# A long 2-D convolution on one Trainium2 core: shifted copies of the input loaded in twelve pieces instead of two

## The chip, the cores and the metric

The kernel runs on one core of a Trainium2 chip (trn2). The metric is the device time of one execution in microseconds (us). The kernel before takes 16334.61 us, the median of three runs (16324.06 to 16345.95). The profile shown below is of one further execution.

The engines are named as the profile names them: PE is TensorE (PEld its weight loads), DVE is VectorE, ACT is ScalarE, POOL is GpSimd, SP is SyncE, which here only issues DMAs. Each engine works through its own list of instructions in the order in which they stand, and an instruction that waits holds up all that stand behind it on that engine.

## The reference

Two residual layers, each on a group-normed input `x` of shape (4, 512, 512, 16), all in float32:

```python
x = x + conv0(gn(x))     # a rational 2-D filter of 512x512 taps, 16 -> 16 channels, by FFT, causal
x = x + conv1(gn(x))     # a 3x3 convolution, cosine-normed, arccos, gated by tanh of norms

def conv0(x, h0, numerators, denumerator):
    h = irfft2(rfft2(pad(numerators)[0]) / rfft2(pad(denumerator)))
    H = h0 + rfft2(h, s=(1024, 1024))
    X = rfft2(x, s=(1024, 1024))
    Y = einsum('...hwi,ijhw->...hwj', X, H)
    return irfft2(Y)[..., :512, :512, :]
```

The change lies in the first layer, in the part that multiplies the two spectra.

## The kernel before

The kernel works in phases: the filter's spectrum, the input's transform along one axis, the **convolution phase** (`conv_phase`, lines 696 to 960), and a last phase with the way back and the second layer. Only the convolution phase is touched. It works through 513 rows, one for each frequency of the first axis (the first frequency counts as two, 0 and the highest). In a row n:

- `load_x`, `load_g` (L748, L736) fetch the row's input `x` (256 KB) and filter `g` (1024 KB).
- `x_part` (L777, PE) turns `x` into 128 frequencies in two pieces of PSUM, `px`, of two images each. Each is copied into `xe[:, 0]` (L727 on DVE or L729 on ACT).
- `x_late` (POOL) stores `xe[:, 0]` into a buffer `xf_d` in device memory (the **first store**, L791, 448 KB), forms a second half `xl` by two pairs of multiplications into `xu` (L798), a multiplication (L799) and an addition (L800), and stores that behind the first (the **second store**, 448 KB). `xf_d` then holds 256 positions by 1024 numbers; there are four such buffers.
- `load_xe` (L815, SP) reads it back as eight copies `xe[:, t]`, copy t shifted by 16 t positions. Copy 0 is there already. Copy 4 is a shift by half and is made by two ACT copies, `half_shift` (L809), the second of them from `xl`. Copies 1 to 3 and 5 to 7 are loaded, in two DMAs of 1536 KB each.
- `g_part` (L829, PE; "pg") turns the filter into `gh`: four groups of 8 matmuls, each group into two PSUM tiles of which there are three buffers, evicted on ACT or DVE.
- `mix` (L845, PE; "pm") multiplies `xe` by `gh`: 128 matmuls in four blocks of 32, each block into a PSUM tile `pm`. There are **two** such buffers; a block is evicted into `yf` by DVE (the first block of a row in the steady state) or ACT (the other three).
- `over_q` (L866, PE; "pz") transposes `yf` in four groups. ACT copies half of a group out (`zq`, L873) and DVE adds and subtracts (five operations, L874 to L878) into `z`. After the fourth group POOL forms `zd` and `z` (L882, L884).
- `over_g` (L903, PE; "py") goes on from there, ACT evicts `yo`, POOL stores it (L914).

`px`, `pz` and `py` share three PSUM buffers. `xe` has three buffers, `xl` one, and `g`, `x`, `gh`, `yf` and `z` two. `evict` (L724 to L729) gives every third PSUM copy to DVE and the others to ACT.

The program text lays these out as a software pipeline (`step`, L923 to L957): in step n it interleaves, quarter by quarter, `mix` of row n, `g_part` of row n+1, `over_q` of row n-1, the second `px` of row n+2 with its `x_late`, `half_shift` of row n+2, the first `px` of row n+3, and `over_g` of row n-2. `load_xe(n + 1)` stands at the head of the step. The text is not the last word on the order, though. A list scheduler decides at build time, from its own estimates of what is ready when, in which order each engine gets its instructions, and the hardware keeps to that order. It also puts each SP DMA on one of eight semaphores in turn, so a DMA waits until the one issued eight earlier has landed. In the kernel before the scheduler has kept the text's interleaving: from row 3 on to the last rows, PE runs one block of 32 mix matmuls, 8 of pg, 4 of pz and then px or py, four times a row.

Of the kernel before, what the change touches and what calls it, by code (L numbers as in the profile page):

```python
# [46 lines left out]
P = 128  # L47
N = 512
B = 4
C = 16  # L50
# [7 lines left out]
XF = F * 2 * B  # L58
XP = XF + 128
# [131 lines left out]
def load_const(nc, pool, cst, name, shape=None):  # L191
    src = cst[name]
    t = pool.tile(list(src.shape), F32, name=f"c_{name}")
    nc.sync.dma_start(out=t, in_=src)
    return t
# [10 lines left out]
def bc(ap, axis, shape):  # L206
    return ap.unsqueeze(axis).to_broadcast(shape)
# [488 lines left out]
def conv_phase(tc, cst, g_d, x_d, y_d):  # L696
    nc = tc.nc
    with ExitStack() as ctx:
# [15 lines left out]
        late = load_const(nc, cp, cst, "late").rearrange("p (v f) -> p v f", v=3)  # L714

        xf_d = [tc.dram_tile([16 * C, XP], F32, name=f"xf_d{n}") for n in range(4)]
# [4 lines left out]
        state = {}  # L721
# [9 lines left out]
        def load_g(n):  # L731
            rc, r, plane = rows[n]
            g = io.tile([P, C, 8 * C], F32, name="g")
            t, w = g.rearrange("p j x -> p (j x)"), C * 8 * C
            if plane is None:
                nc.sync.dma_start(out=t, in_=dram(g_d[rc], r, 0, [GP, P], [1, w]))  # L736
            else:
                for to, at in ((0, (0, 96)[plane]), (64, (64, 32)[plane])):
                    nc.sync.dma_start(out=t[to : to + 32], in_=dram(g_d[rc], r, at * GP, [GP, 32], [1, w]))
                    nc.gpsimd.memset(t[to + 32 : to + 64], 0.0)  # L740
            state["g", n] = g

        def load_x(n):
            rc, r, plane = rows[n]
            x = io.tile([P, B, 8 * C], F32, name="x")
            t, w = x.rearrange("p b x -> p (b x)"), B * 8 * C
            if plane is None:
                nc.sync.dma_start(out=t, in_=dram(x_d[rc], r, 0, [w, P], [1, w]))  # L748
            else:
                nc.gpsimd.memset(t[S:], 0.0)  # L750
                nc.sync.dma_start(out=t[:S], in_=dram(x_d[rc], r, plane * S * w, [w, S], [1, w]))
            state["x", n] = x
# [16 lines left out]
        def x_part(n, b):  # L769

            if b == 0:

                state["xe", n] = xep.tile([P, 8, F, 2, 2, 2], F32, name="xe")
            if b % 2 == 0:
                state["px"] = ps_f.tile([P, 2, F, 2], F32, name="px", tag="full")
            px = state["px"]
            nc.tensor.matmul(px[:, b % 2].rearrange("p f c -> p (f c)"), state["x", n][:, b],  # L777
                             state["dfs", n], start=True, stop=True)
            if b % 2:
                evict(state["xe", n][:, 0, :, b // 2], px.rearrange("p k f c -> p f c k"))  # L780
            if b == B - 1:
                del state["x", n], state["dfs", n]

        def x_late(n):

            xe = state["xe", n][:, 0]
            fl = xe.rearrange("p f h c k -> p f (h c k)")

            def store(half, t):
                at = slice(C, P) if half == 0 else slice(0, P - C)  # L790
                nc.gpsimd.dma_start(out=xf_d[n % 4][half * P :, :XF][at], in_=t[at].rearrange("p f x -> p (f x)"))  # L791

            store(0, fl)
            xl = xlp.tile([P, F, 2, 2, 2], F32, name="xl")
            u = xlp.tile([P, F, 2, 2, 2], F32, name="xu")
            for c in range(2):
                for h in range(2):
                    nc.gpsimd.tensor_mul(u[:, :, h, c], xe[:, :, h, 1 - c], bc(late[:, 1 + c], 2, [P, F, 2]))  # L798
            nc.gpsimd.tensor_mul(xl.rearrange("p f h c k -> p f (h c k)"), fl, bc(late[:, 0], 2, [P, F, 8]))  # L799
            nc.gpsimd.tensor_add(xl.rearrange("p f h c k -> p (f h c k)"),  # L800
                                 xl.rearrange("p f h c k -> p (f h c k)"),
                                 u.rearrange("p f h c k -> p (f h c k)"))
            store(1, xl.rearrange("p f h c k -> p f (h c k)"))
            state["xl"] = xl

        def half_shift(n, half):

            dst, src = ((slice(0, 64), state["xe", n][64:, 0]), (slice(64, P), state["xl"][:64]))[half]
            nc.scalar.copy(state["xe", n][dst, 4].rearrange("p f h c k -> p (f h c k)"),  # L809
                           src.rearrange("p f h c k -> p (f h c k)"))  # L810

        def load_xe(n):
            src = xf_d[n % 4]
            for t in (1, 5):
                nc.sync.dma_start(  # L815
                    out=state["xe", n][:, t : t + 3].rearrange("p t f h c k -> p t (f h c k)"),
                    in_=bass.AP(tensor=src.tensor, offset=src.offset + t * C * XP,
                                ap=[[XP, P], [C * XP, 3], [1, XF]]),
                )

        def g_part(n, j):


            if j % 4 == 0:
                state["pg"] = [ps_g.tile([P, 4, F], F32, name=f"pg{c}", tag="pg") for c in range(2)]
            g, pg = state["g", n], state["pg"]
            for c in range(2):
                half = slice(64 * c, 64 * c + 64)
                nc.tensor.matmul(pg[c][:, j % 4], g[half, j], dg[half], start=True, stop=True)  # L829
            if j == 3:  # L830
                state["gh", n] = ghp.tile([P, F, 2, C], F32, name="gh")
            if j % 4 == 3:
                for c in range(2):
                    evict(state["gh", n][:, :, c, j - 3 : j + 1], pg[c].rearrange("p j f -> p f j"))
            if j == C - 1:
                del state["g", n]

        def mix(n, g):

            if g % 8 == 0:  # L840
                state["pm"] = ps_m.tile([P, 8, 8, 2 * B], F32, name="pm")
            xe, gh, pm = state["xe", n], state["gh", n], state["pm"]
            for q in range(4):
                f = g + 32 * q
                nc.tensor.matmul(  # L845
                    pm[32 * q : 32 * q + 32, g % 8], gh[:, f].rearrange("p c j -> p (c j)"),
                    xe[:, :, f].rearrange("p t h c k -> p t (h c k)"), start=True, stop=True,
                )
            if g == 7:

                state["y", n] = yp.tile([P, 16, 32, 4], F32, name="yf")
            if g % 8 == 7:
                evict(state["y", n][:, :, g - 7 : g + 1].rearrange("p t g x -> p g t x"),
                      pm.rearrange("p g t (h x) -> p g (t h) x", h=2))
            if g == 31:
                del state["xe", n], state["gh", n]
# [65 lines left out]
        def step(n):  # L922


            def row(k):
                return 0 <= n + k < n_rows

            if row(3):
                load_x(n + 3)
            if row(2):  # L930
                load_g(n + 2)
            if row(1):
                load_xe(n + 1)
            for k in range(4):
                if row(0):
                    for g in range(8):
                        mix(n, 8 * k + g)
                if row(1):
                    for j in range(4):
                        g_part(n + 1, 4 * k + j)  # L940
                if row(-1):
                    for t in range(4):
                        over_q(n - 1, 4 * k + t)
                if row(2) and k == 0:
                    for m in range(2, B):
                        x_part(n + 2, m)
                    x_late(n + 2)
                if row(2) and k >= 2:
                    half_shift(n + 2, k - 2)
                if row(3) and k == 1:  # L950
                    turn_x(n + 3)
                if row(3) and k == 3:
                    for m in range(2):
                        x_part(n + 3, m)
                if row(-2) and k in (1, 2):
                    for m in range(2):
                        over_g(n - 2, 2 * (k - 1) + m)  # L957

        for n in range(-3, n_rows + 2):
            step(n)  # L960
# [479 lines left out]
```

## Time and profile before

| what | value |
|---|---|
| median of three runs | 16334.61 us |
| the profiled execution | 16344.5 us, its span on the core 16342.7 us |
| convolution phase, first to last mix matmul | 4654.0 to 13530.0 us: 8876 us for 513 rows, 17.30 us each |
| busy in that stretch | PE 7896.23, PEld 6185.06, DVE 4756.47, ACT 4655.71, POOL 5717.71 us |
| DMA in that stretch | 87% busy on the mean, 328 GB/s |
| granted PE clock in that stretch | 0.98 of full speed |

The profile can be asked for groups of instructions by line, for who waited for whom (what an engine's instruction waited for last, in us, how often, and the longest), for each engine's busy time in stretches, and for a timeline, whose rows give start and duration in us, engine, line, operation, what is written from what, how many alike were put together, and in brackets how long the engine had stood idle and what ended that. In the trace a float32 matmul is two records, so that a block of 32 mix matmuls appears as x64. "issue" means that nothing the profile shows was waited for.

### The profile page before, as it was taken

Reading aid. Unit: us, or ns where it says so; the run is one execution under the profiler, and the core shown is the slowest. Engines: PE = TensorE matmul, PEld = TensorE weight load, DVE = VectorE, ACT = ScalarE, POOL = GpSimd, SP = SyncE. Lnnn points to the kernel's source line nnn. Section 1 sums busy time; section 2 is a strip of 40 time slices with the busy share of each in tenths; the row PEclk is TensorE's granted clock in tenths of the full one; section 3 lists DMA queues with packets and bytes.
Section 4 is the critical chain, followed back from the end, with each engine's and each line's share of the span. In section 5 each row is a group of like instructions: output and inputs, shape, how many; then the busy total and the mean of one; then the engine's idle time right before and its main releaser. Section 6 shows DMA issues by size and latency. Waiting matters only on the chain. (4 is left out here: it accounts for less than half of the span.)

```text
span 16342.7 us, 538107 instructions
## 1 busy us (share of the span) xinstructions
PE 14869.0 (91%) x232588; PEld 10969.0 (67%) x232588; DVE 10396.8 (64%) x20763; ACT 8766.8 (54%) x17007; POOL 10169.4 (62%) x9645
## 2 busy tenths in 40 slices
PE   7999999999988888888888888888888888988888
PEld 5555555554566667766666676667666667877777
DVE  8999999984545555555555555555555552457887
ACT  4666666653345555555555555555555551027888
POOL 7777777763456666666666666666666660247766
PEclk8999999999999999999999999999999999989999
DMA  4888888888878888888888888888888886884531
GB/s 138 239 244 249 241 242 245 245 241 261 250 276 329 323 329 329 329 330 329 329 331 324 330 328 327 328 325 327 330 331 328 326 325 236 319 297 164 168 109 67
DMA packets 2914643, 4542.93 MB, mean 278 GB/s; under 512 B 126114, under 2 KB 2094460, under 8 KB 2801422
## 3 DMA queue, kind: packets, MB, share of 16 engines
q1 hardware_dynamic: 2703070, 3836.37, 67.9%
q0 software_dynamic: 172336, 605.00, 9.3%
q10 hardware_dynamic: 36864, 67.13, 1.2%
q8 instruction: 1831, 30.00, 0.7%
q14 instruction: 542, 4.44, 0.1%
HBM read 3030.71 MB, written 1477.31 MB: 276 GB/s over the span
## 5 line engine op out<-in xcount | busy, mean ns | idle before, releaser
L845 PEld LDWEIGHTS pm<-xe,gh 128*32 128x32 f32 x131328 | 2001.2, 111 | 1446.2 <-issue 1163.4
L845 PE MATMUL pm<-xe,gh 128*32 128x64 f32 x131328 | 2373.7, 222 | 650.1 <-issue 314.8
L829 PE MATMUL pg<-c_dg,g 64*128 64x128 f32 x32832 | 2599.4, 289 | 308.3 <-ACT gh L729 192.5
L874 DVE TENSOR_TENSOR z<-zq,pz 128x256 f32<-128x256 f32 x2052 | 861.6, 420 | 2952.0 <-ACT zq L873 2950.0
L829 PEld LDWEIGHTS pg<-c_dg,g 64*128 64x128 f32 x32832 | 2134.2, 190 | 573.3 <-ACT gh L729 245.9
L729 ACT COPY gh<-pg 128x512 f32<-128x512 f32 x2567 | 1446.9, 585 | 1296.4 <-PE pg L829 1293.9
L459 PE MATMUL pt<-ev_in,c_todd 128*128 128x512 f32 x4096 | 1924.7, 609 | 9.5 <-DMA ev_in<-g_d 9.5
L389 DVE RECIPROCAL dn<-dn 128x256 f32<-128x256 f32 x1024 | 1722.9, 1724 | 17.6
L390 POOL TENSOR_TENSOR sp<-m,dn 128x512 f32<-128x512 f32 x1024 | 1301.2, 1271 | 592.6 <-DVE dn L389 556.1
L809 ACT COPY xe<-xl 64x1024 f32<-64x1024 f32 x513 | 539.0, 1051 | 1883.2 <-POOL xl L800 1883.2
L727 DVE COPY gh<-pg 128x512 f32<-128x512 f32 x1537 | 1056.7, 688 | 663.5 <-PE pg L829 660.3
L866 PE MATMUL pz<-c_ident,yf 128*128 128x128 f32 x8208 | 1376.5, 291 | 19.4 <-issue 13.0
L798 POOL TENSOR_TENSOR xu<-xe,c_late 128x256 f32<-128x256 f32 x2052 | 1373.8, 692 | 20.5 <-DVE xe L727 6.4
L459 PEld LDWEIGHTS pt<-ev_in,c_todd 128*128 128x128 f32 x4096 | 728.9, 190 | 910.3 <-issue 773.0
L418 ACT COPY st<-pg 128x256 f32<-128x256 f32 x2048 | 616.8, 391 | 1301.6 <-PE pg L407 1301.6
L407 PEld LDWEIGHTS pg<-c_dinv,sp 64*128 64x128 f32 x16384 | 1005.6, 196 | 442.2 <-ACT sp L395 232.6
L800 POOL TENSOR_TENSOR xl<-xl,xu 128x1024 f32<-128x1024 f32 x513 | 1208.9, 2357 | 40.2
L407 PE MATMUL pg<-c_dinv,sp 64*128 64x128 f32 x16384 | 1108.3, 287 | 60.3 <-ACT sp L395 44.6
L882 POOL TENSOR_TENSOR zd<-z 128x512 f32<-128x512 f32 x513 | 654.1, 1275 | 781.6 <-DVE z L874 781.6
L903 PE MATMUL py<-z,c_ig 128*64 128x256 f32 x6156 | 1127.4, 397 | 6.6 <-issue 2.2
L1283 PE MATMUL pc<-l_band,xn 128*128 128x160 f32 (+2 forms) x6144 | 1075.8, 333 | 52.0 <-DVE e_o L1338 51.9
L777 PE MATMUL px<-dfs_n,x 128*128 128x256 f32 x4104 | 1080.4, 387 | 12.7 <-DMA c_late<-k_late 11.5
(211 smaller groups left out, 29585.0 us busy)
## 6 DMA issues: line engine op xcount, KB each, us to landing
xe<-xf_d SPq DMA_DIRECT2D x1026, 1536.0 KB
g<-g_d SPq DMA_DIRECT2D x511, 1024.0 KB
g_d<-st SPq DMA_DIRECT2D x256, 1024.0 KB
ev_in<-g_d SPq DMA_DIRECT2D x1024, 256.0 KB
g_d<-ot SPq DMA_DIRECT2D x1024, 256.0 KB
xf_d<-xe POOLq DMA_DIRECT2D x513, 448.0 KB, 8.3
xf_d<-xl POOLq DMA_DIRECT2D x513, 448.0 KB, 6.4
x_d<-xo SPq DMA_DIRECT2D x128, 1024.0 KB
```

Source lines behind the costliest of these rows:

```text
L389: nc.vector.reciprocal(dn, dn)
L390: nc.gpsimd.tensor_mul(w["sp"][:, v], w["m"][:, v], bc(dn, 2, [P, 2, 2, P]))
L407: nc.tensor.matmul(pg[u][:, n, k].rearrange("p a x -> p (a x)"), w["sp"][q, n, k, c, :], dinv[q, 2 * kp + k, c, :], start=(c == 0), stop=( ...
L459: nc.tensor.matmul(pt, todd[:, c, kc, hh * P : hh * P + P], ev[:, kc, c], start=(kc == 0), stop=(kc == 1),)
L729: nc.scalar.copy(dst, src)
L777: nc.tensor.matmul(px[:, b % 2].rearrange("p f c -> p (f c)"), state["x", n][:, b], state["dfs", n], start=True, stop=True)
L798: nc.gpsimd.tensor_mul(u[:, :, h, c], xe[:, :, h, 1 - c], bc(late[:, 1 + c], 2, [P, F, 2]))
L800: nc.gpsimd.tensor_add(xl.rearrange("p f h c k -> p (f h c k)"), xl.rearrange("p f h c k -> p (f h c k)"), u.rearrange("p f h c k -> p (f ...
L829: nc.tensor.matmul(pg[c][:, j % 4], g[half, j], dg[half], start=True, stop=True)
L845: nc.tensor.matmul(pm[32 * q : 32 * q + 32, g % 8], gh[:, f].rearrange("p c j -> p (c j)"), xe[:, :, f].rearrange("p t h c k -> p t (h c k ...
L866: nc.tensor.transpose(pz[:, t % 4].rearrange("p v q x -> p (v q x)"), y[:, at].rearrange("p g x -> p (g x)"), ident)
L903: nc.tensor.matmul(py[64 * half : 64 * half + 64, odd], ig[:, s0, c2], zs.rearrange("p (t h) j -> p h t j", h=2), start=(c2 == 0), stop=(c ...
```

## The change

Copy t of `xe` at position p is position 16 t + p of `xf_d`. Positions below 128 come from the first store, the others from the second. The changed `load_xe` cuts every copy there: for each t the partitions below 128 - 16 t are one DMA, the others another one. That makes six early DMAs (112, 96, 80, 48, 32 and 16 partitions of 4 KB) and six late ones (16 to 112 partitions), 1536 KB in either set. The late ones stay at the head of the step, for row n+1; the early ones go into the last quarter of the step before, for row n+2 there. What is computed is the same.

```diff
-        def load_xe(n):
-            src = xf_d[n % 4]
-            for t in (1, 5):
+        def load_xe(n, late):
+            for t in (1, 2, 3, 5, 6, 7):
+                cut = P - t * C
+                p = slice(cut, P) if late else slice(0, cut)
                 nc.sync.dma_start(
-                    out=state["xe", n][:, t : t + 3].rearrange("p t f h c k -> p t (f h c k)"),
-                    in_=bass.AP(tensor=src.tensor, offset=src.offset + t * C * XP,
-                                ap=[[XP, P], [C * XP, 3], [1, XF]]),
+                    out=state["xe", n][p, t].rearrange("p f h c k -> p (f h c k)"),
+                    in_=xf_d[n % 4][t * C + p.start : t * C + p.stop, :XF],
                 )
...
             if row(1):
-                load_xe(n + 1)
+                load_xe(n + 1, True)
             for k in range(4):
...
                     x_late(n + 2)
+                if row(2) and k == 3:
+                    load_xe(n + 2, False)
                 if row(2) and k >= 2:
                     half_shift(n + 2, k - 2)
```

With the change the scheduler also arrives at another order on PE, ACT and DVE. The order on POOL stays the same, row for row.

## Prediction

> **What bounds the kernel now.** I read the page first, then the convolution phase alone (4654 to 13530 us): its busy times, then who waited for whom on PE and on SP. PE is busy 7896.23 of 8876 us, 15.4 of 17.30 us a row. Of its idle time, these are the large parts:
>
> ```profile
> PE pm L845 <- issue: 314.8, 260, 3.6
> PE pm L845 <- DMA xe<-xf_d: 251.6, 155, 2.8
> PE pg L829 <- ACT gh L729: 191.4, 218, 3.7
> PE pg L829 <- issue: 109.4, 106, 2.1
> ```
>
> The reader is to see that mix waits for the loads the change touches, but only 251.6 us in all, 0.5 us a row. SP's own waits say why the loads are late:
>
> ```profile
> SPq L815 <- DMA xf_d<-xl: 6930.3, 512, 15.9
> ```
>
> SP stands 13.5 us of each row before the loads until the second store has landed. The change aims at this. So the kernel is bound by PE, with a ring of stores and loads almost as long beside it.
>
> **What it removes.** Half the bytes can go before the second store, so the late half is shorter: at most the 251.6 us, plus the 35.4 and 15.7 us in which mix is put down to DVE operations long done. That is 0.6 us a row, 300 us.
>
> **What it adds on SP.** Ten more issues a row. An xe issue takes 0.40 us (median), so twelve take 4.8 us, in the 13.5 us that SP stands idle. Behind the early pieces' wait for the first store stand x(n+4), g(n+3) and the late pieces. x and g are used two rows later, the late pieces too (below), so they have over 17 us; if that cover were gone, mix would wait as it does now, about 0.5 us a row. The eight semaphores make the fourth early piece wait for the second late one of the row before, issued a row earlier: nothing. Bytes stay at 3072 KB a row, in runs of 4 KB as before. What an issue of 16 to 112 partitions does to the rate no row shows; nearest are the present loads (328 GB/s over the phase) and the phase's poorest 4 us (160 GB/s). I take the present rate, and keep half of it for a rival.
>
> [...]
>
> **What it moves: the order on PE, ACT and DVE.** This decides. I read the order of both built programs. Before, PE has mix in four blocks with pg, pz, px, py between. After, all 513 rows have mix as one run of 128, behind everything else of the row. Two kinds of round alternate from the end of mix(m) to the end of mix(m+1), "#" being the number of a group:
>
> ```
> PE   A: pg(m+1) 7 left | pz(m-1)#4 | px(m+3)#1 | pz(m)#1 | px(m+3)#2 | pz(m)#2 |
>         pg(m+2) 16 | py | pg 8 | pz(m)#3 | py | pg 8 | mix(m+1) 128
> PE   B: pz(m-1)#4 | px(m+3)#1 | pz(m)#1 | half px(m+3)#2 | pg(m+2) 8 | half px |
>         pg 8 | pz(m)#2 | py | pg 8 | pz(m)#3 | py | pg 1 | mix(m+1) 128
> POOL  : zd,z(m-1) | xu xu | first store(m+3) | xu xu | xl | xl add | second store
> ACT   : ... L809 xe<-xl(m+3) | gh#5 | zq(m)#3 | yo | (A: gh#8) | yf(m+1)#2,3,4
> DVE   : ... L874-L878 (m)#3 | (A: gh#7) | yf(m+1)#1
> ```
>
> Mix has two PSUM buffers: its third block waits for yf#1 on DVE. That stands behind L874 of group 3, which waits for zq on ACT, which stands behind L809, which waits for POOL's xl; and that chain starts only after the last mix, with pz#4. So a row is now one ring through five engines. Its POOL part, from a row of before:
>
> ```profile
> 9015.70 0.42 DVE L874 TENSOR_TENSOR z<-zq,pz 128x256 f32<-128x256 f32 x1
> 9016.21 1.27 POOL L882 TENSOR_TENSOR zd<-z 128x512 f32<-128x512 f32 x1 [1.32 <-DVE z L874]
> 9017.56 1.27 POOL L884 TENSOR_TENSOR z<-z 128x512 f32<-128x512 f32 x1
> 9018.80 1.32 POOL L798 TENSOR_TENSOR xu<-xe,c_late 128x256 f32<-128x256 f32 x2
> 9021.01 0.68 DVE L727 COPY xe<-px 128x512 f32<-128x512 f32 x1
> 9021.99 0.57 POOL L791 DMA_DIRECT2D xf_d<-xe  x1 [1.87 <-DVE zq L875]
> 9022.59 1.34 POOL L798 TENSOR_TENSOR xu<-xe,c_late 128x256 f32<-128x256 f32 x2
> 9023.88 1.98 POOL L799 TENSOR_TENSOR xl<-xe,c_late 128x1024 f32<-128x1024 f32 x1
> 9025.93 2.35 POOL L800 TENSOR_TENSOR xl<-xl,xu 128x1024 f32<-128x1024 f32 x1
> 9028.31 1.04 ACT L809 COPY xe<-xl 64x1024 f32<-64x1024 f32 x1 [3.72 <-POOL xl L800]
> ```
>
> From the end of L874 (9016.12) to the end of the second xu pair is 4.0 us; from the store's issue (9021.99) to the end of the addition (9028.28) 6.3 us. Today mix(k) goes on beside it.
>
> The same jam stands in the trace already: at the phase's start (rows 0 to 2) this order was used:
>
> ```profile
> 4668.87 2.00 PE L845 MATMUL pm<-xe,gh 128*32 128x64 f32 x128
> 4670.78 2.34 POOL L800 TENSOR_TENSOR xl<-xl,xu 128x1024 f32<-128x1024 f32 x1
> 4673.15 1.04 ACT L809 COPY xe<-xl 64x1024 f32<-64x1024 f32 x1 [4.26 <-POOL xl L800]
> 4674.21 1.07 ACT L729 COPY yf<-pm 128x512 f32<-128x512 f32 x2
> 4674.85 0.65 PE L845 MATMUL pm<-xe,gh 128*32 128x64 f32 x15 [3.98 <-ACT yf L729]
> 4675.73 1.59 PE L845 MATMUL pm<-xe,gh 128*32 128x64 f32 x49 [0.23 <-issue]
> 4679.02 1.94 PE L845 MATMUL pm<-xe,gh 128*32 128x64 f32 x64
> ```
>
> Two blocks, then PE idle 3.98 us until ACT, held by POOL, evicts one; and afterwards a block takes 1.94 us, not the usual 1.10.
>
> **The sum for a row**, from the end of mix(m) at 0. Start to start, a mix block takes 1.03, 8 pg 1.10, half a px 0.48; pz lasts 0.66; zq takes 0.07 + 0.37, L874 0.04 + 0.42, the five together 1.6; a semaphore back to PE 0.2.
>
> - A: 7 pg 0.97, pz 1.63, zq 2.07, L874 2.53; POOL 4.0 + 6.3 gives 12.83 (xe#2 is ready at 5.6, in time). L809 0.03 and 1.07 to the next ACT start: gh#5 starts at 13.92, zq 0.48 later, ends 14.79; DVE's five 16.42; gh#7 and yf#1, 0.69 each, 17.8; PE 18.0; two blocks: **20.06**.
> - B: pz 0.66; zq waits for yf#4, 1.03; L874 1.5. px#2 needs pz#4's PSUM buffer (2.9), has 8 pg in its middle and ends at 5.0; xe#2 5.75, store issue 6.05, addition 12.34; gh#5 13.44, zq ends 14.3, the five 15.93, yf#1 16.6, PE 16.8, two blocks: **18.86**.
>
> Mean 19.46. The second store lands at about 20 (landing 6.4 us, the page's median) and mix(m+3) starts two rows later: the loads, the change's object, are far off the ring. Two costs come on top. PE has by then done the rest of its list. A: px#2 4.9, pz 5.4, pg 6.5, pg 8.4 (held 0.9 by ACT's gh behind the first L809), py 9.4, pg 10.5, pz, py 12.1; B: px#2 and pg 4.9, pg 6.1, pz, py 7.7, pg 8.8, pz, py, one pg 10.45, two mix blocks 12.5. So it stands idle in A from 12.1 to 14.7 and in B from 12.5 to 16.8. After such pauses the trace has slow matmuls: two blocks 3.08 for 2.06 us after 3.77 us idle, one 2.4 for 1.03 after 3.98, and 1.36 for 1.03 after 2.34. I take 1.3 us in B, 0.4 in A, mean 0.85; bounds 0 and 3.0 (all 3.7 us of PE work on the ring at 1.8 times). And PE's "issue" pauses, 424 us or 0.83 a row, count for the quarter of PE's work on the ring: 0.2, bounds 0 and 0.83. Together **20.5 us a row**, 3.2 more, times 513 is 1642; on 16344.5 that is 17986, and less the 10 us by which the profiled execution lies above the median, **17980 us**.
>
> [...]
>
> **Rivals.**
> - *Faster: the ring does not close.* If POOL's chain from L874 took under about 7 us instead of 10.3, gh#5 and yf#1 would be done when PE gets there. Then PE's own list decides: A 12.1 + 0.96 + 4.1 = 17.2, B 10.45 + 4.1 = 14.6, mean 15.9, with issue pauses 16.5: 0.8 less a row, **15920**. For it: the DMA wait does go, the second store has two rows of time. Against it: POOL's chain is there, op by op, with the same order.
> - *No change*, the ring costing what the DMA wait gave, 17.3 us a row: **16335**. It takes a ring 2 us shorter than its measured links.
> - *The pieces bound.* At half the rate, 3.1 MB at 160 and 2.5 MB at 328 GB/s take 27 us a row: **21300**. Against it: the runs stay 4 KB and many pieces are in flight.
> - *Ring, dearer or cheaper than its bounds*: under 18.9 or over 21.9 us a row.
>
> **How the numbers follow.** The ring within 18.9 to 21.9 us a row (17150 to 18700) 0.78, outside it but slower 0.08, pieces 0.05, faster 0.07, no change 0.02. So slower by over 0.2% (33 us, about what a measurement of this kernel can tell from no change) 0.91, within 0.02, faster 0.07. The range 17150 to 18700 is the ring's: below, its links alone, a little shorter than summed; above, links with most of both extra costs.
>
> **What would show it.** PE's wait for DMA xe near nothing; instead mix waiting for DVE (yf, or L878 before it) and pg for ACT gh, some 4 us a row together; ACT's wait at L809 for POOL longer than today's 3.7 us a row; rounds alternating, near 20.5 each; granted clock below 0.98; DMA below 300 GB/s. Wrong if mix waits for DMA, if rounds are under 18 us, or if POOL's operations change their lengths.

## The result and the profile after

The changed kernel takes 19655.99 us, the median of four runs (19630.93 to 19690.53), against 16337.76 us before. The ratio is 1.2033 (95% interval 1.2013 to 1.2054), 3318 us or 6.5 us more in each of 513 rows. Slower was right. The size was not: 17980 us was predicted, with 18700 as the upper end.

The page of the changed kernel, its granted PE clock, DMA share and rate:

```profile
PEclk8999999998888888888888889888988888998999
DMA  5888888888999999899999999999999999697441
GB/s 153 245 244 244 240 245 247 251 251 227 235 241 243 242 243 243 227 237 235 243 239 242 234 239 241 242 238 238 246 238 234 240 243 233 226 325 244 158 138 70
```

The reader is to see that the DMA engines are busier than before (9 tenths for 8) while they move a quarter less per second: about 240 GB/s in the convolution phase, where it was 328. A busy share says how long packets were under way, not how much they carried. The bytes are the same.

What PE waited for in the convolution phase after (4700 to 16800 us; total, times, longest, in us):

```profile
PE pm L845 <- issue: 1349.5, 499, 8.2
PE pm L845 <- DVE yf L727: 657.7, 226, 6.5
PE pg L829 <- ACT gh L729: 470.7, 503, 4.0
PE px L777 <- DVE z L878: 265.1, 300, 1.2
```

The wait for the loads (251.6 us before) is gone, as the change meant. The forecast ring is there: mix waits for yf, pg for gh. But the largest item is one that I had put at 0.2 us a row on the ring: pauses in which PE waits for nothing that the profile shows. Two ends of rounds in the timeline of after, both in mix, show the two kinds:

```profile
10001.34 2.00 PE L845 MATMUL pm<-xe,gh 128*32 128x64 f32 x128
10002.99 1.05 ACT L809 COPY xe<-xl 64x1024 f32<-64x1024 f32 x1 [4.24 <-POOL xl L800]
...
10006.46 0.68 DVE L727 COPY yf<-pm 128x512 f32<-128x512 f32 x1
10007.20 1.50 PE L845 MATMUL pm<-xe,gh 128*32 128x64 f32 x46 [3.86 <-DVE yf L727]
...
10027.63 3.00 PE L845 MATMUL pm<-xe,gh 128*32 128x64 f32 x182
10035.38 2.34 PE L845 MATMUL pm<-xe,gh 128*32 128x64 f32 x74 [4.74 <-issue]
```

The first is the ring, link by link: two blocks (x128), then PE stands 3.86 us until yf; and ACT, from which the chain to yf goes by zq and DVE, stood 4.24 us at L809 until POOL's addition. The second cannot be a wait for an eviction. It falls after 182 records, inside the third block of 64, and no new PSUM tile begins there.

### The profile page after: what moved, and what is told of

It reads as the page before. It is cut to its first block, busy times and chain, and to the rows that moved or that the text cites. A ratio compares the mean times of both kernels' runs of the same rounds, so it can differ in the third digit from the quotient of the medians.

```text
span 19660.4 us, 549094 instructions
## 1 busy us (share of the span) xinstructions
PE 16114.9 (82%) x232588; PEld 12084.8 (61%) x232588; DVE 11232.9 (57%) x20763; ACT 8899.2 (45%) x17007; POOL 10148.6 (52%) x9645
## 5 line engine op out<-in xcount | busy, mean ns | idle before, releaser
L845 PE MATMUL pm<-xe,gh 128*32 128x64 f32 x131328 | 2638.2, 245 | 2022.5 <-issue 1357.6
L845 PEld LDWEIGHTS pm<-xe,gh 128*32 128x32 f32 x131328 | 2375.8, 126 | 2240.4 <-issue 1450.4
L829 PE MATMUL pg<-c_dg,g 64*128 64x128 f32 x32832 | 3055.7, 301 | 578.0 <-ACT gh L729 487.0
L829 PEld LDWEIGHTS pg<-c_dg,g 64*128 64x128 f32 x32832 | 2544.5, 201 | 1386.4 <-ACT gh L729 668.4
L729 ACT COPY yf<-pm 128x512 f32<-128x512 f32 x1538 | 907.8, 590 | 2936.9 <-PE pm L845 2936.5
L777 PE MATMUL px<-dfs_n,x 128*128 128x256 f32 x4104 | 1376.1, 454 | 365.6 <-DVE z L878 265.1
L866 PE MATMUL pz<-c_ident,yf 128*128 128x128 f32 x8208 | 1496.7, 311 | 105.5 <-issue 97.6
L866 PEld LDWEIGHTS pz<-c_ident,yf 128*128 128x128 f32 x8208 | 1060.7, 157 | 395.7 <-issue 194.1
L903 PE MATMUL py<-z,c_ig 128*64 128x256 f32 x6156 | 1195.5, 410 | 4.2 <-DVE z L877 2.3
L809 ACT COPY xe<-xl 64x1024 f32<-64x1024 f32 x513 | 536.5, 1046 | 1420.8 <-POOL xl L800 1420.8
```

The lines of the kernel that those rows point to most:

```text
L729: nc.scalar.copy(dst, src)
L845: nc.tensor.matmul(pm[32 * q : 32 * q + 32, g % 8], gh[:, f].rearrange("p c j -> p (c j)"), xe[:, :, f].rearrange("p t h c k -> p t (h c k ...
L866: nc.tensor.transpose(pz[:, t % 4].rearrange("p v q x -> p (v q x)"), y[:, at].rearrange("p g x -> p (g x)"), ident)
L903: nc.tensor.matmul(py[64 * half : 64 * half + 64, odd], ig[:, s0, c2], zs.rearrange("p (t h) j -> p h t j", h=2), start=(c2 == 0), stop=(c ...
```

## The experiments

Since the change moves both the loads and the order, I separated them. In the kernels whose order was "held", the order of all instructions of the phase on PE, DVE, ACT and POOL was written into the program, as the built kernel before or after has it, and only the loads differ.

**1. The loads alone.** Loops of 48 repeats that only load, in the old form (L287), as twelve pieces (L291), as six whole copies (L295), as twelve halves by columns (L299) and others. All other work is left out.

> Loads alone: the two layers are left out, and so is every engine's work but one small copy on VectorE a repetition; the output is part of the input. Eight loops of 48 repetitions, each repetition filling one of three buffers with 3072 KB from four buffers in device memory: (1) the two DMAs of before, (2) the twelve pieces, the early set and then the late one, (3) six whole copies of 128 partitions, (4) twelve DMAs of 128 partitions by half a row (2 KB), (5) the early set twice, (6) the late set twice, (7) the twelve pieces, early and late piece of a copy in turn, (8) twenty-four DMAs into the lowest 16 partitions (1536 KB). Theory 'narrow transfers clog': the time of a repetition goes by which partitions are being written at the same time. 1, 3 and 4 alike, about 9 us (3072 KB at the 350 to 410 GB/s of the busiest stretches of before); 2, 5 and 6 about 1.7 times that, by the 294 ns that a 4 KB packet takes in the changed kernel against 173 before; 7 near 1; 8 by far the lowest rate. Theory 'number of transfers': 4, 2 and 7 alike and slow, 3 between, 5 and 6 like 2. Theory 'the loads are as fast as before and only the order of the engines matters': all of 1 to 7 about 9 us.

The groups of that kernel, whose last figure is DVE's idle time until a loop's loads had landed:

```profile
L299 DVE COPY mark<-xe 128x3 f32<-128x3 f32 x48 | 8.1, 169 | 379.6 <-DMA xe<-xf_d 379.6
L295 DVE COPY mark<-xe 128x3 f32<-128x3 f32 x48 | 8.1, 169 | 362.7 <-DMA xe<-xf_d 362.7
L291 DVE COPY mark<-xe 128x3 f32<-128x3 f32 x48 | 8.1, 169 | 738.8 <-DMA xe<-xf_d 738.8
L287 DVE COPY mark<-xe 128x3 f32<-128x3 f32 x48 | 8.1, 169 | 387.4 <-DMA xe<-xf_d 387.4
L311 DVE COPY mark<-xe 128x3 f32<-128x3 f32 x48 | 8.1, 169 | 615.5 <-DMA xe<-xf_d 615.5
```

Divided by 48, with the copy's 0.17 us, a row's 3072 KB take 15.6 us in the twelve pieces, 7.7 in six whole copies, 8.1 in twelve DMAs over all 128 partitions, and 13.0 when early and late pieces of a copy take turns (L311). The two loads come to 8.2 by the same division, but their loop is the first and holds the start of the program: its first copy waits until the buffers in device memory have been filled.

```profile
34.21 0.17 DVE L287 COPY mark<-xe 128x3 f32<-128x3 f32 x1 [33.34 <-DMA xe<-xf_d]
```

The 47 repeats behind it take 7.7 us each. So the pieces run at half the rate. Their number doesn't do that, as twelve DMAs over all partitions show. What is left is that each piece reaches only a part of the partitions.

**2. The order without the pieces.** The two loads of before, the order of after held:

```diff
+            tc.add_manual_dep(mine[b], mine[a].name, dep, reason="given order")
```

> The kernel before with its two large loads, but PE, VectorE, ScalarE and GpSimd are given, instruction for instruction, the order of the changed kernel in the convolution phase. Theory 'ring', my prediction's: the order alone costs the predicted 3.2 us a row, 20.5 us, so about 17980 us, with PE waiting for the eviction of mix and for gh; then the 3.3 us a row that the changed kernel takes above that is the pieces' own. Theory 'the loads': the order costs little, 16340 us. Theory 'the order is all': 19650 us as the changed kernel.

18704.13 us, ratio 1.1439 (1.1420 to 1.1458): 4.6 us a row more. PE's waits in 5000 to 13000 us:

```profile
PE pm L867 <- DVE yf L749: 679.4, 183, 6.6
PE pg L851 <- ACT gh L751: 479.6, 363, 4.0
PE pm L867 <- issue: 386.4, 171, 4.7
```

(L867 is mix; the lines shift by 22.) The ring stands here by itself, with the loads of before: the order alone makes what I forecast, 20.5 us a row, and 1.4 us more.

**3. The pieces without the order.** The change's loads, the order of before held.

> The changed kernel with its twelve pieces, but PE, VectorE, ScalarE and GpSimd are given, instruction for instruction, the order of the kernel before in the convolution phase. Theory 'ring': mix no longer waits for the loads (0.6 us a row less than before), about 16050 us. Theory 'narrow transfers clog': the DMA engines are busy over 90% for 22.4 us a row, as in the changed kernel, and that bounds the row: 18900 to 19600 us, mix waiting for DMA and PE standing in issue pauses of more than 2 us a row. Theory 'both add': about 18000 us.

18876.87 us, ratio 1.1544 (1.1527 to 1.1561), 4.9 us a row more. The page's DMA row of that kernel:

```profile
DMA  4888888877999999999999999999999999696432
```

and PE's waits in 5000 to 13000 us, some 360 rows:

```profile
PE pm L867 <- issue: 1270.6, 523, 6.1
...
PE pm L867 <- DMA xe<-xf_d: 26.1, 11, 5.3
```

A row is 22.2 us, and the DMA engines are busy 0.97 to 0.98 of it in four windows of 200 us. That fits experiment 1: they were busy 0.87 of 17.3, or 15.1 us, before, and 7.9 more makes 23.0, an estimate somewhat above the 21.6 measured. So the order alone costs 2345 us and the pieces alone 2518, and together they cost 3318, not the sum.

The surprise is how it shows: PE hardly waits for a load, but at mix alone 3.5 us a row (1270.6 over 360) for "issue". I looked at what these pauses end with. The page shows a DMA queue for instructions whose packets hold 16 KB each:

```profile
q8 instruction: 1835, 30.06, 0.7%
```

Of 618 such pauses of PE over 1 us between 6000 and 14000 us, the middle 90% end 1.27 to 1.73 us after the end of such a packet, although one comes only every 7.9 us. I read this as PE standing without instructions until the next packet has come; what the traces show is the timing. In the changed kernel, the pauses over 1 us in the last two mix blocks of a round behave alike: 255 of them, half over 3.8 us, the middle 90% ending 1.29 to 1.74 us after a packet. So do those with the order alone (2), where the DMA engines are only 0.70 busy: 166 of them, 1.23 to 1.56 us after a packet. The order thus makes such pauses by itself. That full DMA engines bring the packets late, and so lengthen the pauses, is argued from experiment 7, where half the bytes shorten them; no run delays the packets alone.

**4. Twelve broad loads.** Each copy's load cut by columns, 2 KB a partition, all of them behind the second store by their data.

```diff
+                h = slice(XF // 2, XF) if late else slice(0, XF // 2)
...
+                    in_=xf_d[n % 4][t * C : t * C + P, h],
```

> The changed kernel, but the twelve DMAs are cut by columns instead of partitions: each copy in two halves of 2 KB a partition on all 128 partitions; all need both stores. The scheduler then keeps the order of before on PE. Theory 'narrow transfers clog': as before within 1%, 16200 to 16500 us. Theory 'number of transfers': 18000 us or more. Theory 'order is all': as before, 16340 us.

16911.50 us, ratio 1.0342 (1.0327 to 1.0358); the order on PE stayed that of before. Mix waits 507.9 us for the loads in 5000 to 13000 us, where before waits 233.5. The expectation that twelve broad DMAs cost nothing falls in the kernel, but twelve with 2 KB runs cost 1.1 us a row, not 6.5. Six of them also stand earlier in SP's list than the loads of before, so the 1.1 us need not be the count's alone.

**5. Which partitions.** Loads alone again, 1536 KB a repeat in runs of 4 KB, in eight forms.

```diff
+    def middle(xe, src):
+        for t in T:
+            piece(xe, src, t, 32, 96)
```

> The loads alone, as in the measurement of the load forms: eight loops of 48 repeats, each repeat 1536 KB in runs of 4 KB, no other work, the output is only a copy of x. In order: three DMAs of 128 partitions; six of the partitions 0 to 63; six of 32 to 95; six of 64, low and high half in turn; twelve of 0 to 31; twenty-four of 16, over all eight groups in turn; twenty-four of 0 to 15 whose source rows lie 8 apart; three of 128 partitions that all read one and the same row. Place theory (the partitions that a DMA reaches set its rate, since every DMA goes through the same queue and is worked off one after another): 128 partitions about 4.1 us a repeat (half of the 8.2 us that 3072 KB took); 0 to 63 about 7.7 to 8.2; 32 to 95 different from 0 to 63 although it has as many partitions. [...] Both halves in turn 8 if the DMAs go one after another, 4 if side by side. Size theory (a DMA of 64 partitions is slow because it is small): the three forms of 64 partitions take the same time, about 7.7. Source theory (rows that lie close together in device memory are slow to read): the one row is much slower than 4.1, and the sixteen partitions with rows 8 apart are much faster than the 42 us that sixteen low partitions took with neighbouring rows; by the other two theories they take 42 again and the one row 4.1.

The groups, by line: L298 is 128 partitions, L302 0 to 63, L306 32 to 95, L310 the halves in turn, L314 0 to 31, L318 sixteen over all groups in turn, L322 the low sixteen, L326 one row. The last figure is again DVE's idle time:

```profile
L298 DVE COPY mark<-xe 128x3 f32<-128x3 f32 x48 | 8.1, 169 | 203.9 <-DMA xe<-xf_d 203.9
L326 DVE COPY mark<-xe 128x3 f32<-128x3 f32 x48 | 8.1, 169 | 194.9 <-DMA xe<-xf_d 194.9
L310 DVE COPY mark<-xe 64x3 f32<-64x3 f32 x48 | 8.0, 166 | 316.8 <-DMA xe<-xf_d 316.8
L302 DVE COPY mark<-xe 64x3 f32<-64x3 f32 x48 | 7.7, 160 | 357.5 <-DMA xe<-xf_d 357.5
L318 DVE COPY mark<-xe 32x3 f32<-32x3 f32 x48 | 7.7, 160 | 526.4 <-DMA xe<-xf_d 526.4
L306 DVE COPY mark<-xe 32x3 f32<-32x3 f32 x48 | 7.7, 159 | 179.0 <-DMA xe<-xf_d 179.0
L322 DVE COPY mark<-xe 16x3 f32<-16x3 f32 x48 | 7.5, 156 | 1907.1 <-DMA xe<-xf_d 1907.1
L314 DVE COPY mark<-xe 32x3 f32<-32x3 f32 x48 | 7.5, 156 | 957.3 <-DMA xe<-xf_d 957.3
```

Compare L302 with L306: same number of DMAs, same size, same buffer, and 64 partitions either way. Partitions 32 to 95 take 3.9 us, 0 to 63 take 7.6. All 128 take 3.9 as well (L298 without its first repeat, which holds the start of the program). So it is the place, and not the size. The DMA engines are busy throughout in both loops (their share is 1.04 in 230 to 575 us and 1.03 in 590 to 760 us), but a 4 KB packet takes 325 ns on the mean for partitions 0 to 63 and 163 ns for 32 to 95. One row read by all 128 partitions is about as fast (L326, 4.2 us), so rows that lie close together are not what is slow.

Both halves in turn take 6.8 us, nearer to the 7.6 of DMAs worked off one after another than to 3.9. That fits early and late pieces in turn, which still take 13.0 us (1). How slow a piece of 16 or of 112 partitions is by itself, no run measures.

The loops of 32 and 16 partitions (L314, L318, L322) show no rate. In L314 and L322 two and four DMAs in a row write the same partitions of a copy, and SP waits for one to land before it issues the next (in L322 1319.7 of the 1700 us from 2700 to 4400 us); the DMA engines are only 0.35 and 0.16 busy. In L318 nothing is written twice, but 24 issues in 11.1 us are one every 0.46 us, near the 0.40 us that an issue takes, with the engines 0.54 busy. So the far rows of L322 don't test the source theory. The 42 us of sixteen low partitions, which the expectation took as a rate, came from a loop of the same kind.

**6. The ring cut.** The order of after held, with one instruction moved on ACT, L809 of `xl` from ahead of gh#5 to behind zq#4 and the xe copy. First with the loads of before, then with the pieces.

```
ACT, as held:   ... L809 xe<-xl | gh#5 | zq#3 | yo | yf yf yf | gh#8 | zq#4 | xe ...
ACT, changed:   ... gh#5 | zq#3 | yo | yf yf yf | gh#8 | zq#4 | xe | L809 xe<-xl ...
```

> The loads of before and the order of after on PE, DVE, ACT and POOL, with one instruction moved: the second half shift (L809, xe from xl) stands on ACT behind zq of group 4 and the xe copy, not ahead of gh 5 and zq of group 3. Ring theory (mix's third block waits through yf, L874, zq and L809 for POOL's chain): the ring is cut, PE's own list decides again, 16 to 17.3 us a row, 15900 to 16700 us, and mix waits for DVE yf under 1 us a row. Rival, that the order itself costs (mix as one run of 128 over two PSUM buffers, with long pauses of clock and fetch): about 18700 as with the half shift in its place.

17648.58 us, ratio 1.0793 (1.0777 to 1.0809), between what the two theories gave. PE's waits in 5000 to 13000 us:

```profile
PE pm L867 <- issue: 637.5, 403, 5.0
PE pg L851 <- ACT gh L751: 468.2, 386, 1.6
```

Mix's wait for DVE's yf, 679.4 us with L809 in its place, is 0.3 us here. The ring is shown, and cutting it is worth 1056 us (18704.13 less 17648.58), or 2.1 us a row. The other 1298 us of the order are not the ring: they lie in the pauses, in pg's wait for gh, and in a clock of 0.95. With the ring cut this order runs 19.9 us a row, where my "faster" rival put PE's list alone at 16.5.

> The changed kernel with the same one instruction moved on ACT. Theory of two limits (DMA engines saturated by the pieces at about 22.3 us a row, the ring at about 21.9, together 23.8 because they disturb each other): with the ring cut the DMA engines alone set the row, 22.2 to 22.4 us, 18800 to 19000 us, DMA 0.99 busy. If the ring is what sets the changed kernel and the pieces only stretch it, 16700 or less. If neither, 19650 as now.

19513.83 us, ratio 1.1936 (1.1905 to 1.1967): only 142 us less than the changed kernel, where I expected 700. With the pieces the ring is not what limits. But the DMA engines, at 0.92 to 0.99 in four windows of 200 us, don't explain 23.4 us a row alone either.

**7. The pieces at half their bytes.** The order of after held, every piece loads 512 of its 1024 columns, and mix reads these twice. The other half is left out. The same was done with the two loads of before.

```diff
-                    xe[:, :, f].rearrange("p t h c k -> p t (h c k)"), start=True, stop=True,
+                    xe[:, :, f % 64].rearrange("p t h c k -> p t (h c k)"), start=True, stop=True,
```

> The changed kernel, its order held fixed on PE, DVE, ACT and POOL, but every piece loads only the first half of its columns (2 KB a partition instead of 4 KB, 1536 KB a row), and mix reads that half twice; the second half is left out. Number of DMAs, their partitions, the waits and all other work are those of the changed kernel. Theory: the pieces lengthen the row by keeping the DMA engines busy 22.3 us a row, which also delays the fetch of PE's instructions; with some 7 us of that gone, the row falls to the ring as the loads of before leave it (21.9 us a row, 18700 us), PE's pauses with nothing waited for in the last two mix blocks fall from 2.1 to about 1.0 us a round, and DMA is below 0.75 busy. Rival: the number of DMAs and their waits on SP (not the time that they take) is what costs: 19650 as now. Rival: the pauses have nothing to do with DMA traffic: the links get shorter by about 0.5 us a row, the pauses stay at 2.1, 19400.

> The two broad loads of before in the order of after, held fixed, and each load brings only the first half of the columns (1536 KB a row, 2 KB a partition), mix reading that half twice; the second half is left out. With all columns this took 18704 us, 21.9 us a row, with 1.0 us of it in pauses of PE in which nothing was waited for and 0.6 us more in the links than I had summed (DMA 0.70 busy). If DMA traffic makes both, they shrink: pauses 0.5 us or less, links 0.3, so 20.9 us a row, 18200 us. If the pauses come from the order (mix's many instructions in one run) and the links from the engines themselves, 18700 as before.

The pieces: 18425.96 us, ratio 1.1267 (1.1234 to 1.1300), 1230 us less than with all bytes. The broad loads: 18690.08 us, ratio 1.1429 (1.1395 to 1.1462), no different from 18704.13. The page's DMA row of the pieces at half their bytes:

```profile
DMA  4888888887666666666666666666666665796431
```

and PE's waits there in 5000 to 13000 us:

```profile
PE pm L867 <- DVE yf L749: 700.7, 187, 6.5
...
PE pm L867 <- issue: 262.2, 163, 4.6
```

Twelve narrow DMAs cost nothing beyond the time that they take: relieved of half of it, the row is the ring again, at 21.3 us. SP's waits for earlier pieces to land go with it, though, so what these waits cost by themselves isn't shown. In the changed kernel they are 3.3 us a row:

```profile
SPq L816 <- DMA xe<-xf_d: 1700.7, 1472, 3.8
```

With broad loads at 0.70 busy, relief gives nothing. So DMA time costs here only where the engines are near full (0.89 to 0.96 in the changed kernel in four windows of 200 us), and the pauses that the order makes by itself stay.

**8. Can the kernel before be helped?** From what the profile said of ACT (3.7 us a row at L809), I moved L809 of `xl` behind the last yf in the order of before, held; and I split its two loads into six whole copies, alone and together with that. The reason for the split, 7.7 us against 8.2 in experiment 1, was none: without the start of the program the two loads take 7.7 us too.

> The kernel before with its own order, and the second half shift (L809, xe from xl) moved on ACT behind the last yf of the row, so that gh, zq and yf no longer stand behind ACT's wait for POOL (3.7 us a row). If that wait costs PE anything (pg waiting for gh 191 us in all, and what follows it), 16000 to 16250; if PE is bound by its own list and by the loads, 16300 to 16360.

> The kernel before in its own order, held fixed, with the two loads of three copies each split by copies only: six loads of 512 KB, each over all 128 partitions, all behind the second store as before. Alone, six such loads took 7.7 us where the two took 8.2. Place theory (partitions reached count, not the number of DMAs): within 0.3% of before, 16300 to 16390 us, DMA 0.87 busy. Rival (more DMAs over the same queue and eight semaphores cost time by themselves, as the twelve halves by columns at 16912 us might say): 16600 or more.

> The same six loads, and the second half shift moved on ACT behind the last yf of the row, as in the run that did only that (16393 us: pg's wait for gh went, mix's wait for the loads grew by as much). If the loads' own length is what mix waits for there, six shorter loads let some of that through: 16150 to 16300. If mix waits for the second store's landing, not for the length of the loads: 16340 to 16400.

16392.52 us, ratio 1.0026 (1.0017 to 1.0036); 16570.91 us, 1.0126 (1.0109 to 1.0143); 16611.21 us, 1.0154 (1.0139 to 1.0169). None beats the kernel before. In the first, pg's wait for gh (176.7 us in 5000 to 13000 us) is gone, and mix's wait for the loads has risen from 233.5 to 381.3: the gain was handed on to the next wait. In the second, which lies between what its two theories gave, the wait for loads falls to 162.0 but the pauses rise from 273.4 to 454.9. No run here points to a version that beats both kernels.

## Why the prediction was right in direction and wrong in size

I took the period from the end of one mix to the next apart, as the prediction's sum does, from the traces (means of A and B, in us, over the rounds from 5000 to 15000 us, in the changed kernel to 16000). Slow running is what the last two blocks take beyond 2.06 us without their pauses; a pause is a gap over 0.3 us in them:

| term | predicted | order alone (2) | changed kernel |
|---|---|---|---|
| links, to the third mix block | 17.4 | 18.08 | 18.63 |
| two blocks at full speed | 2.06 | 2.06 | 2.06 |
| slow running after the pause | 0.85 | 0.79 | 1.02 |
| pauses of "issue" on the ring | 0.2 | 1.02 | 2.08 |
| **sum** | **20.5** | **21.95** | **23.79** |

- **What bounds before; what is removed.** Right. Mix's wait for the loads is gone. But at 0.5 us a row it was a small item.
- **The ring.** Right, and shown by cutting it (6). PE's third block starts at 18.9 in A and 17.3 in B with the order alone, where 18.0 and 16.8 were summed. The largest part of that 0.7 is POOL, whose addition ends at 13.3 and 13.0 for 12.8 and 12.3.
- **SP's issues.** Right as far as shown: ten more issues cost nothing themselves (7). SP's waits for earlier pieces, put at nothing, are 3.3 us a row; they come from the slow pieces and go with them.
- **The clock.** Right: 0.79 for 0.85, and 0.3 in A and 1.25 in B where I took 0.4 and 1.3. With the order alone PE stands 3.8 us before B's third block, and the granted clock is 0.5 for a part of the last two blocks in 95% of these rounds; in the changed kernel it is so in 116 of the 120 rounds (5000 to 16000 us) in which more than 3 us lie before that block.
- **The pauses.** Failed. "PE's 'issue' pauses ... count for the quarter of PE's work on the ring: 0.2, bounds 0 and 0.83". I spread a mean of before over PE's work. In the new order they sit on the ring, in the last blocks of every other round: 2.0 us there in A, none in B. Even the order alone is above my upper bound of 0.83, and with it the time, 18704.13 us, stands at the upper end of the range.
- **The rate of the pieces.** Failed, and this is the step that put the time well outside the range. "What an issue of 16 to 112 partitions does to the rate no row shows ... I take the present rate, and keep half of it for a rival." The present rate, for loads alone, is 408 GB/s; the pieces' is 202 (1). Half was the truth. The rival at 0.05 priced it at 27 us a row from the phase's poorest 4 us. Worked out from the load forms it is an estimated 23.0, and 22.2 measured (3), beside a ring of 20.5: near enough for the two to disturb each other. "The runs stay 4 KB and many pieces are in flight" was a reason about size and number, where place decides: six DMAs of 256 KB took 3.9 us or 7.6, by their partitions (5).
- **What would show it.** Clock, DMA rate and the waits for yf and gh came as said; these two and the wait at L878 make 2.7 us a row, not 4. ACT's wait at L809 fell, to 2.7 us a row from 3.7: ACT itself arrives later.

How the two costs add up in the changed kernel is shown only in part. With full DMA engines the pauses are longer (2.1 for 1.0) and so are the links (18.6 for 18.1), and halving the bytes takes that back (7). What stays open: why the pieces without the ring still take 23.4 us a row when they take 22.2 in the order of before; why pieces at half their bytes have shorter pauses (0.7 us a round) than broad loads at half theirs (1.05); and what sets the place of a pause. That PE has many short instructions to fetch where mix runs as one stretch of 128 may be the reason for the order's own pauses. It wasn't tried.

## What to carry to other kernels

Cutting a transfer along partitions may double its time though bytes and runs stay equal (here 15.6 us a row for 7.7, loads alone): measure the new form alone before costing it at the old rate, and look at what else uses the same DMA engines, PE's instructions among them (the queue of 16 KB packets in 3). A dependence removed from a load may also reorder everything, since the scheduler builds from its own estimates; hold the order to tell the two apart. When a wait with no releaser appears inside a run of matmuls, look for instruction packets, not for data (here the pauses ended 1.2 to 1.7 us after one).

## What the runs showed of the hardware

Loads from device memory, 4 KB runs, alone (5): 128 partitions 3.9 us for 1536 KB, 32 to 95 3.9, 0 to 63 7.6, both halves in turn 6.8. In the changed kernel's convolution phase a 4 KB packet of the queue of SP's loads took 294 ns on the mean, in that of the kernel before 174. PE's pauses of "issue" end 1.2 to 1.7 us after a 16 KB packet of the instruction queue, with full DMA engines and without (3). Why partitions 0 to 63 take longer than 32 to 95, no run shows.
